# A two-layer hybrid model on one core: where the second batch's projection stands in a list of side work

## Chip, core and metric

The kernel runs on one core of a Trainium2 chip. The metric is device time in microseconds (us); shown are the median, the lowest and the highest of the runs of a kernel. A profiled execution gives the trace: every instruction with its start and duration, the DMAs, and the clock that TensorE was granted. Engines are named as in the profile: PE is TensorE's matmuls, PEld its weight loads, DVE VectorE, ACT ScalarE, POOL GpSimd, SP the queue that issues most DMAs.

## What is computed

The input x is 2 batches of 1024 tokens of width 128, held as 16 tiles of 128 tokens (tiles 0 to 7 are batch 0, 8 to 15 batch 1). Eight blocks are applied one after the other, each as x = x + block(layernorm(x)). The last four matter here; the change lies in the seventh and eighth:

```python
x = x + _L1_attn_a_ref(_layernorm(x, axis=-1), ...)   # linear attention
x = x + _L1_ffn_ref(_layernorm(x, axis=-1), Wg, Wu, Wd)
x = x + _L1_attn_b_ref(_layernorm(x, axis=-1), ...)   # the head softmax
x = x + _L1_ffn_ref(_layernorm(x, axis=-1), Wg, Wu, Wd)
```

The head softmax has 16 heads of 8 dimensions, and its softmax runs over the heads (axis 1), not over the keys:

```python
dp = jnp.einsum('bhqd,bhkd->bhqk', q, k) * SCALE
attn = jax.nn.softmax(dp, axis=1)
w_avg = jnp.einsum('bhqk,bhkd->bhqd', attn, v)
```

The expert block sums, over 8 experts, (silu(x Wg) * (x Wu)) Wd with a middle width of 512. It works token by token, so any group of tokens can be done as soon as their own input is final. The head softmax mixes the tokens of one batch and needs the keys and values of the whole batch.

## The kernel before, in words

`first_layer` does the first five blocks and, beside the end of them, the expert block for tokens of batch 0. `experts_ffn(g, w, [2])` does it for tiles 8 to 11. Then comes `heads_and_experts(g, w, [6, 7], [0, 1, 2, 3, 4, 5])`, and last `experts_ffn(g, w, [3])`, the eighth block for tiles 12 to 15.

**The loop.** `heads_and_experts` walks over 128 blocks: batch b, tile of queries qb, tile of keys kb, the keys innermost (L1120). The order of instructions on every engine is the order of the calls (`manual_schedule`). Work on a block is spread over five iterations of the loop at L1137, which runs i from -1 to 131:

- L1030 (PE): the scores of all 16 heads for block i+1, into h_s.
- L1041 and L1047 (DVE): the largest score over the heads, and the scores less it, into h_e.
- L1050 (ACT): the exponentials in place, in two halves.
- L1056 (DMA from SP) and L1060 (adding DMA from POOL): the upper eight heads are added on the lower eight in flight, giving h_e2. (The page gives both names as h_e.)
- L1065 (PE): the eight sums are added up by matmuls with the identity, into h_pd. L1070 (DVE): the reciprocal.
- L1075 (POOL): h_a = exponentials times reciprocal. L1081 (PE): the weighted values into h_po.

After the eighth key tile of a query tile the result is copied (L1176), projected (L1145) and added to x (L1154), and `finished` goes up by one.

**The expert stream.** In the same iterations runs the expert block on chunks of two tiles (`ExpertStream`). Chunks 6 and 7 (tiles 12 to 15) still belong to the sixth block, and the head softmax of batch 1 needs them; chunks 0 to 5 (tiles 0 to 11) belong to the eighth and need the head softmax of their own tiles. Opening a chunk is five steps: statistics (L62, L63 on DVE), root (L66, ACT), inverse (L69, DVE), application (L73, POOL), and transposes (L863, PE), which put 32 units, one for each expert and quarter of the middle width, into `ex.units`. In each iteration `ex.products()` takes two units and multiplies by Wg and Wu (L879), `ex.gates()` does the silu (L886, ACT), and in the next iterations `ex.multiply()` (L894, DVE), `ex.outputs()` (L905, PE) and `ex.add()` (L914, DVE) finish them. L905, L1145 and L1065 share one bank, h_pd, which has a single buffer.

**The projection.** `preparation(b)` normalizes the eight tiles of batch b and makes its queries, keys and values. Its steps are four of statistics and an inverse (DVE), a root (ACT), four applications (L73, POOL), eight on PE (two each of transposes L986, keys L1001, queries L992, values L1007, each with what follows on ACT or DVE) and two biases (L979, POOL). Batch 0's is done ahead of the loop, beside chunk 6. Batch 1's has to be done by the time block 64 begins: its scores are issued in iteration 63, and `spread(1)` (L1023) at the end of iteration 66 uses its values.

**The list.** `side` is an ordered list of such openings and the projection of batch 1. Each entry has a number that `finished` has to reach. `aside(place)` is called four times in an iteration, with "pe", "act", "dve" and "pool", and does the next step of the current entry if it belongs to that place. When an entry is used up, the next is taken only if `finished` has reached its number and `ex.units` holds no more than 8 units. A step of place "pe" stands in place of `ex.products()`: in such an iteration no units are taken. Nothing in the list overtakes.

After the loop, a `while` loop (L1179) takes what is left, two units in a round, with nothing beside them.

Of the kernel before, what the change touches and what calls it, by code (L numbers as in the profile page):

```python
# [927 lines left out]
def heads_and_experts(g, w, first, second):  # L928
# [4 lines left out]
    with ExitStack() as es:  # L933
# [24 lines left out]
        ex = ExpertStream(g, w, ework, ps_e)  # L958
        qzs, kTs, vs = {}, {}, {}

        def preparation(b):

            xb = g.x[:, b * TPB : (b + 1) * TPB, :]
            ln = StagedNorm(g, xb, TPB, "h")
            u = seq.tile([P, TPB, D], F32, name="h_u", bufs=1)
            uT = seq.tile([P, L], F32, name="h_uT", bufs=1)
            qzs[b] = seq.tile([P, K, L], F32, name="h_qz")
            kTs[b] = seq.tile([P, L], F32, name="h_kT")
            vs[b] = seq.tile([P, TPB, D], F32, name="h_v", bufs=1)
            for t in range(0, TPB, 2):  # L970
                yield "dve", lambda t=t: ln.stats((t, t + 1))
            yield "act", ln.root
            yield "dve", ln.inverse
            for t in range(0, TPB, 2):
                yield "pool", lambda t=t: ln.apply(u, (t, t + 1))


            def bias(t):
                nc.gpsimd.tensor_add(  # L979
                    xb[:, t : t + 4, :], xb[:, t : t + 4, :], w["b_proj2"].unsqueeze(1).to_broadcast([P, 4, D])  # L980
                )

            def transposes(n):
                pt = ps_e.tile([P, 4, P], F32, name="e_pgu")
                for t in range(4):
                    nc.tensor.transpose(pt[:, t, :], u[:, 4 * n + t, :], g.ident)  # L986
                nc.scalar.copy(uT[:, bass.ts(n, 512)], pt.rearrange("p a b -> p (a b)"))

            def query(n):
                cols = bass.ts(n, 512)  # L990
                pm = ps_e.tile([P, 4, P], F32, name="e_pgu").rearrange("p a b -> p (a b)")
                nc.tensor.matmul(pm, w["w_qkv2"][:, 0:P], uT[:, cols], start=True, stop=True)  # L992
                for k in range(K):
                    nc.scalar.activation(  # L994
                        qzs[b][:, k, cols], pm, AF.Identity, bias=keep_b[:, k : k + 1], scale=keep[:, k : k + 1]
                    )

            def key(n):
                cols = bass.ts(n, 512)
                pm = ps_e.tile([P, 4, P], F32, name="e_pgu").rearrange("p a b -> p (a b)")  # L1000
                nc.tensor.matmul(pm, w["w_qkv2"][:, P : 2 * P], uT[:, cols], start=True, stop=True)  # L1001
                nc.scalar.activation(kTs[b][:, cols], pm, AF.Identity, bias=w["b_qk2"][:, 1:2])

            def value(n):
                pv = ps_e.tile([P, 4, P], F32, name="e_pgu")
                for t in range(4):
                    nc.tensor.matmul(  # L1007
                        pv[:, t, :], uT[:, bass.ts(4 * n + t, P)], w["w_qkv2"][:, 2 * P : 3 * P], start=True, stop=True
                    )
                nc.vector.tensor_add(  # L1010
                    vs[b][:, 4 * n : 4 * n + 4, :], pv, w["b_v2"].unsqueeze(1).to_broadcast([P, 4, D])
                )

            for step in (transposes, key, query, value):
                for n in range(2):
                    yield "pe", lambda step=step, n=n: step(n)
            for t in (0, 4):
                yield "pool", lambda t=t: bias(t)
# [69 lines left out]

        side = [(2 * c + 2, ex.opening(c)) for c in second]
        side.insert(2, (0, preparation(1)))
        side = [(0, ex.opening(c)) for c in first[1:]] + side
        finished, current, head = 0, None, None

        def aside(place):

            nonlocal current, head
            while True:
                if head is None:  # L1100
                    if current is None:
                        if not side or side[0][0] > finished or len(ex.units) > 8:
                            return False
                        current = side.pop(0)[1]
                    head = next(current, None)
                    if head is None:
                        current = None
                        continue
                break
            if head[0] != place:  # L1110
                return False
            step, head = head[1], None
            step()
            return True
# [7 lines left out]
        with tc.manual_schedule(engines=ALL):  # L1122
# [14 lines left out]
            for i in range(-1, n + 4):  # L1137
# [9 lines left out]
                if not aside("pe"):  # L1147
                    ex.products()
# [3 lines left out]
                if oT is not None:  # L1152
                    xt = g.x[:, finished, :]
                    nc.vector.tensor_add(xt, xt, pd[:, 2, :])  # L1154
                    finished, oT = finished + 1, None
                aside("act")
                ex.gates()
                if i + 1 < n:
                    e_[i + 1] = exponentials(heads, m)
                    e2_[i + 1] = lower(e_[i + 1])  # L1160
                aside("dve")
                if 0 <= i - 1 < n:
                    d_[i - 1] = denominators(e2_.pop(i - 1))
# [115 lines left out]
def kernel(ctx: ExitStack, tc: tile.TileContext, d: dict, out: bass.AP):  # L1279
# [36 lines left out]
    layer0.close()  # L1316
    experts_ffn(g, w, [2])
    heads_and_experts(g, w, [6, 7], [0, 1, 2, 3, 4, 5])
    experts_ffn(g, w, [3])

# [67 lines left out]
```

## Time and profile before

| what | value |
|---|---|
| median of 3 runs (lowest to highest) | 2319.74 us (2317.05 to 2331.03) |
| profiled execution: its own time | 2328.53 us |
| profiled execution: span of its instructions | 2326.8 us |
| busy in the span: PE, DVE, ACT, POOL | 2015.9, 1629.0, 1183.5, 854.9 us |
| loop of the head softmax: first to last L1041 | 1307.8 to 2190.2 us |
| last expert stage: its first transpose (L96) | 2237.37 us |
| the part from 1308 us on, of the span | 1019 us |

The span is counted from the first instruction to the last; 1.7 us of the execution lie around it. All times of single instructions below are of the profiled execution, in us from the start of its span. The head softmax with its loop and the last expert stage are somewhat under half of the span. A busy PE is not PE at its peak, since the ends of matmuls are modelled, but a gap in it is a gap.

### The profile page before, as it was taken

To read this page: it belongs to the slowest core of one execution; us is meant where nothing else is said; L and a number is where in the kernel's file an instruction comes from. 1 tells how busy PE (TensorE), PEld (TensorE's weight loads), DVE (VectorE), ACT (ScalarE), POOL (GpSimd) and SP (SyncE) were. 2 spreads that over 40 slices of the span, in tenths; PEclk is the share of its full clock that TensorE was granted. 3 is DMA by queue.
4 is the path that set the end of the run, shared out by engine and by line. 5 is a ranking of instruction groups with operands and counts; after the bars stand their busy time and mean duration, and the time that the engine had idled before them with its cause. 6 is when DMAs were issued, how large, how long until landed. Compare 5 with 4: busy or idle time off the path is not lost. (4 is left out here: it accounts for less than half of the span.)

```text
span 2326.8 us, 36810 instructions
## 1 busy us (share of the span) xinstructions
PE 2015.9 (87%) x15152; PEld 1184.5 (51%) x15152; DVE 1629.0 (70%) x1988; ACT 1183.5 (51%) x1486; POOL 854.9 (37%) x460
## 2 busy tenths in 40 slices
PE   7779988887987748789698799999977999999999
PEld 4323344323334313235345577677755777777754
DVE  5851047788974659993423699899978999999732
ACT  1014521353643458764322576777735777777632
POOL 0001100033320000000102277878788787877700
PEclk9789997878998879899799899999989999999999
DMA  3000000076732067640000266566556665665500
GB/s 86 1 1 1 2 1 1 18 190 152 185 93 89 4 159 184 162 106 0 1 1 0 64 153 157 145 152 157 146 150 152 157 155 155 153 162 146 137 5 5
DMA packets 72647, 220.19 MB, mean 95 GB/s; under 512 B 9056, under 2 KB 19744, under 8 KB 72352
## 3 DMA queue, kind: packets, MB, share of 16 engines
q1 hardware_dynamic: 53584, 149.40, 21.5%
q0 software_dynamic: 18432, 67.12, 15.3%
q8 instruction: 119, 1.95, 0.3%
q10 hardware_dynamic: 464, 1.33, 0.3%
q14 instruction: 48, 0.39, 0.1%
HBM read 78.35 MB, written 5.24 MB: 36 GB/s over the span
## 5 line engine op out<-in xcount | busy, mean ns | idle before, releaser
L1075 POOL TENSOR_TENSOR h_a<-h_e,h_r 128x2048 f32<-128x2048 f32 x128 | 581.4, 4542 | 130.4 <-PE h_po L1081 93.9
L1041 DVE TENSOR_REDUCE h_m<-h_s 128x128 f32<-128x2048 f32 x128 | 293.2, 2291 | 73.2 <-PE h_s L1030 73.1
L1065 PE MATMUL h_pd<-h_e,ident 128*128 128x128 f32 x2048 | 267.4, 285 | 43.4 <-DMA h_e<-h_e 29.6
L1050 ACT ACTIVATE h_e<-h_e 128x1024 f32<-128x1024 f32 x256 | 256.5, 1049 | 89.6 <-DVE h_e L1047 71.4
L1047 DVE TENSOR_TENSOR h_e<-h_s,h_m 128x2048 f32<-128x2048 f32 x128 | 292.6, 2286 | 3.4 <-DVE h_m L1041 1.7
L1065 PEld LDWEIGHTS h_pd<-h_e,ident 128*128 128x128 f32 x2048 | 244.6, 196 | 87.3 <-DVE x_res L914 41.5
L304 POOL TENSOR_SCALAR_AFFINE_SELECT a_pT<-a_pT 128x256 f32<-128x256 f32 x128 | 97.2, 775 | 431.4 <-ACT a_pT L301 430.5
L301 ACT ACTIVATE a_pT<-a_st 128x1024 f32<-128x1024 f32 (+1 forms) x192 | 145.1, 808 | 139.1 <-PE a_st L291 137.0
L886 ACT ACT_TABLE_LOAD x105 | 134.7, 1283 | 150.5 <-PE e_pgu L879 150.3
L806 DVE TENSOR_TENSOR e_h<-e_sg,e_pu 128x512 f32<-128x512 f32 x128 | 87.0, 686 | 176.5 <-PE e_pu L802 151.2
L243 DVE TENSOR_REDUCE a_nm<-a_s 128x2 f32<-128x1024 f32 (+7 forms) x144 | 168.4, 1218 | 48.5 <-PE a_s L234 24.2
L804 ACT ACTIVATE e_sg<-e_pg 128x512 f32<-128x512 f32 x128 | 76.0, 596 | 192.5 <-PE e_pg L801 192.3
L825 PE MATMUL e_po<-e_h,Wd 128*128 128x512 f32 x256 | 139.4, 630 | 39.4 <-DVE e_h L806 39.3
L225 PE MATMUL a_s<-a_latT,a_qT 32*128 32x512 f32 (+3 forms) x768 | 128.7, 650 | 49.4 <-DVE a_nm L243 47.6
L905 PEld LDWEIGHTS h_pd<-Wd,e_h 128*128 128x128 f32 x1024 | 125.5, 191 | 90.1 <-DVE e_h L894 76.8
L1030 PE MATMUL h_s<-h_qz,h_kT 32*128 32x512 f32 x1024 | 148.5, 649 | 19.5 <-DVE h_e L1047 13.9
L879 PE MATMUL e_pgu<-e_uT,Wg 128*128 128x256 f32 x512 | 154.1, 383 | 4.0 <-ACT h_qz L994 2.1
L905 PE MATMUL h_pd<-Wd,e_h 128*128 128x128 f32 x1024 | 149.1, 287 | 5.9 <-DVE e_h L894 3.7
L879 PE MATMUL e_pgu<-e_uT,Wu 128*128 128x256 f32 x512 | 152.3, 379 | 0.0
L1060 POOL DMA_DIRECT2D h_e<-h_e x128 | 113.6, 887 | 104.0 <-DVE h_m L1041 48.8
L638 DVE TENSOR_TENSOR_SCAN s_h<-s_a,s_h 128x1024 f32<-128x1024 f32 x64 | 147.4, 2303 | 5.9 <-ACT s_a L606 1.7
L801 PE MATMUL e_pg<-e_uT,Wg 128*128 128x512 f32 x256 | 141.9, 638 | 2.1 <-ACT e_uT L794 2.1
(246 smaller groups left out, 3191.6 us busy)
## 6 DMA issues: line engine op xcount, KB each, us to landing
h_e<-h_e SPq DMA_DIRECT2D x128, 512.0 KB, 4.0
h_e<-h_e POOLq DMA_DIRECT2D x128, 512.0 KB, 4.6
s_a<-s_steps SPq DMA_DIRECT2D x64, 512.0 KB, 4.8
s_h<-s_steps SPq DMA_DIRECT2D x64, 512.0 KB, 6.3
s_steps<-s_delta SPq DMA_DIRECT2D x4, 512.0 KB, 2.6
s_steps<-s_dtx SPq DMA_DIRECT2D x4, 512.0 KB, 3.4
Wg<-in_Wg_dram SPq DMA_DIRECT2D x8, 256.0 KB, 6.0
Wu<-in_Wu_dram SPq DMA_DIRECT2D x8, 256.0 KB, 5.9
```

The costliest lines, as they stand in the source:

```text
L243: nc.vector.tensor_reduce(nm[:, half, i, h : h + together], s[:, :, :n], AX.X, ALU.max, negate=True)
L301: nc.scalar.activation(pT[:, :, off:], s[:, :, off:], AF.Exp)
L638: nc.vector.tensor_tensor_scan(h, a, h, 0.0, ALU.mult, ALU.add)
L801: nc.tensor.matmul(pg, w["Wg"][:, e, f], opened[n], start=True, stop=True)
L879: nc.tensor.matmul(pgu[:, k, :], w[name][:, e, f], uT, start=True, stop=True)
L905: nc.tensor.matmul(po[:, t, :], h[:, bass.ts(t, P)], self.w["Wd"][:, e, fc, :], start=(k == 0), stop=(k == 1))
L1030: nc.tensor.matmul(s[:, j, :].rearrange("p (k q) -> p k q", k=K), kTs[b][quad, bass.ts(kb, P)], qzs[b][quad, :, bass.ts(qb, P)], start=Tru ...
L1041: nc.vector.tensor_reduce(m, heads.rearrange("p h q -> p q h"), AX.X, ALU.max)
L1047: nc.vector.tensor_sub(e, heads, m.unsqueeze(1).to_broadcast([P, H, P]))
L1050: nc.scalar.activation(eh, eh, AF.Exp, scale=scale)
L1065: nc.tensor.matmul(pd, g.ident, e2[:, k, :], start=(k == 0), stop=(k == 7))
L1075: nc.gpsimd.tensor_mul(a, e, r.unsqueeze(1).to_broadcast([P, H, P]))
```

## The change

Each entry of the list gets a second number, the units that may be left over when it is taken (it was 8 for all). The projection of batch 1 moves from behind chunk 1 to behind chunk 0, and its number is 24; all openings keep 8.

```diff
-        side = [(2 * c + 2, ex.opening(c)) for c in second]
-        side.insert(2, (0, preparation(1)))
-        side = [(0, ex.opening(c)) for c in first[1:]] + side
+        side = [(2 * c + 2, 8, ex.opening(c)) for c in second]
+        side.insert(1, (0, 24, preparation(1)))
+        side = [(0, 8, ex.opening(c)) for c in first[1:]] + side
...
-                        if not side or side[0][0] > finished or len(ex.units) > 8:
+                        if not side or side[0][0] > finished or len(ex.units) > side[0][1]:
                             return False
-                        current = side.pop(0)[1]
+                        current = side.pop(0)[2]
```

So the list was: chunk 7, chunk 0 (from 2 finished tiles on), chunk 1 (from 4), projection, chunks 2 to 5 (from 6, 8, 10, 12). It becomes: chunk 7, chunk 0 (from 2), projection with up to 24 units left, chunk 1 (from 4), chunks 2 to 5 as before. The instructions are the same; their places in the loop differ.

## Prediction

> **What bounds the kernel now.** I read the page first. Its chain of waits over the whole span is spread over many stages, so it does not say what a list of side work is worth. The groups then show which engine each part of the head softmax occupies, and from there I went to the stage itself: busy time by stretches, the timeline of single iterations, and the chain in the last 150 us.
>
> Busy time of each engine in stretches (columns: busy us and instruction counts of PE, PEld, DVE, ACT, POOL; granted TensorE clock; DMA share; GB/s):
>
> ```profile
> 1480.00:1660.00 180.00, 176.59 (x1861) 136.18 (x1860) 164.41 (x162) 134.98 (x158) 140.72 (x55) 1.00 0.60 153
> 1709.00:1726.00 17.00, 11.83 (x116) 8.76 (x116) 10.87 (x7) 4.57 (x6) 12.84 (x7) 0.76 0.54 135
> 1726.00:1782.00 56.00, 43.67 (x478) 31.39 (x478) 44.95 (x28) 23.80 (x31) 45.07 (x19) 0.92 0.56 147
> 2224.00:2237.00 13.00, 12.25 (x78) 11.04 (x76) 6.09 (x15) 3.28 (x9) 0.00 (x0) 1.00 0.00 0
> ```
>
> The first line is the loop with expert units in every iteration: PE is busy 98% at full clock. The second and third are where the loop has run out of units and only the projection of the second batch stands beside it: PE falls to 70 and 78%, and the clock to 0.76 and 0.92. The fourth is after the loop: PE alone, no DMA, POOL idle. I call iterations with units loaded and those without light. Iteration i (from -1) is found by its L1041, which works on block i+1; "row i" is the time from its L1041 to the next.
>
> A loaded iteration in the timeline:
>
> ```profile
> 1967.07 1.16 PE L905 MATMUL h_pd<-Wd,e_h 128*128 128x128 f32 x8
> 1968.07 0.60 PE L879 MATMUL e_pgu<-e_uT,Wg 128*128 128x256 f32 x2
> 1969.88 2.05 PE L1065 MATMUL h_pd<-h_e,ident 128*128 128x128 f32 x16
> 1971.86 1.08 PE L1081 MATMUL h_po<-h_a,h_vz 128*32 128x128 f32 x32
> 1972.88 1.14 PE L1030 MATMUL h_s<-h_qz,h_kT 32*128 32x512 f32 x8
> 1973.94 1.16 PE L905 MATMUL h_pd<-Wd,e_h 128*128 128x128 f32 x8
> ```
>
> From L905 to L905 is 6.87 us with no gap: 1.0 outputs, 1.8 units (L879), 2.0 denominators, 1.0 weighing, 1.1 scores. PE sets the loaded row. A light one, with one projection step:
>
> ```profile
> 1740.02 1.13 PE L1001 MATMUL e_pgu<-h_uT,w_qkv 128*128 128x512 f32 x2
> 1742.24 2.02 PE L1065 MATMUL h_pd<-h_e,ident 128*128 128x128 f32 x16 [1.10 <-DMA h_e<-h_e]
> 1744.19 1.08 PE L1081 MATMUL h_po<-h_a,h_vz 128*32 128x128 f32 x32
> 1745.20 1.14 PE L1030 MATMUL h_s<-h_qz,h_kT 32*128 32x512 f32 x8
> ```
>
> Here 6.27 us pass, with PE waiting 1.10 for the sum in flight (h_e by DMA): DVE's 5.5 us of two reductions and a reciprocal, and that DMA, set the light row. So 2.8 us of expert work put into a light row costs only 6.87 - 6.1 to 6.3 = 0.6 to 0.8 us. After the loop the same work is bare; the chain shows one such round, 2.62 us (2226.34 to 2228.96):
>
> ```profile
> 2226.34 0.89 PE h_pd L905 x8
> 2227.23 1.73 PE e_pgu L879 x8
> 2228.96 0.89 PE h_pd L905 x8
> ```
>
> **What the change does, counted.** I ran the list by hand with the rules of the code (two units an iteration, a step of place "pe" in their stead, `finished` one up every eight). Before, chunk 1 is opened at i=35 and fed from i=38, the projection starts at i=50 when 8 units are left, they end at i=54, and i=55 to 69 have none: 15 light iterations. Chunk 2 waits for the projection, and so each chunk after it. Chunk 5 comes to PE at i=117 and 10 of its units are left when the loop ends at i=131. The traces confirm each of these places (L879 stops and starts there). After: chunk 0 is open at i=21, its 24th unit from the end is reached at i=25, and the projection runs i=25 to 41 (statistics 25 to 28, root 29, applications 29 to 32, eight PE steps 33 to 40, biases 40 and 41). Only i=33 to 40 have no new units; the 10 left resume at i=41, chunk 1 opens at i=42 with 6 left, and from there no chunk is late. The last unit goes at i=130. Five loaded iterations more, none of the five bare rounds.
>
> **The moved steps, priced.** No instruction is added or removed, none of the moved steps issues a DMA, and SP's issues keep their order with the blocks; what moves on SP is the write of the first 512 rows, ready some nine rows later, in a loaded row. The second such write, at 2045 in a loaded row of 6.88, cost nothing, so I take nothing (if SP stalled on it, the h_e copies would queue behind it: up to 1 us).
>
> Rows 50 to 71 of before hold projection and refill: 6.99, 7.19, 6.99, 7.07, 6.88, 6.87, 6.88, 10.22, 6.90, 8.26, 6.12, 6.27, 6.73, 8.10, 7.78, 6.10, 6.75, 6.74, 6.40, 6.86, 6.92, 6.36, in all 155.4. The same 22 roles after are rows 25 to 46; each takes the nearest row of before:
> - 25 to 29, statistics (four instructions, 0.9 us of DVE, hidden behind PE but for 0.12) and the root, already in loaded rows before: 6.99, 6.99, 7.19, 6.99, 6.88 = 35.0.
> - 30 to 32, applications on POOL, now beside units. POOL then has 0.88 + 1.6 to 2.0 + 4.52 = 7.0 to 7.4 against 6.87; behind them on POOL stands the next h_a, which PE's L1081 waits for. 6.95, 6.95, 7.0 = 20.9 (7.4 each would add 1.3).
> - 33 and 34, transposes while outputs drain, as rows 55 and 56: 6.9 each.
> - 35, first key step with a finished tile: 6.6 (row 67 has 6.74 with statistics).
> - 36 to 40, as 61 to 65: 6.3, 6.7, 8.1, 7.8, 6.1. The 8.1 and 7.8 stay: L1010 stands before L1041 on DVE and waits for PE.
> - 41 to 46, refill and opening of chunk 1, as rows 1 (5.96, here with a bias of 1.56 on POOL), 3, 36, 37, 38, 39, where a kind has several rows their middle: 6.5, 6.9, 7.2, 7.0, 6.9, 6.2.
> In all 152.0. Elsewhere before has four openings in loaded rows (chunks 1, 3, 4, 5) and after too (2 to 5), and 80 rows of the same kinds: **the loop -3.4**. The bounds are -8 (no stall at all) and +2 (stalls like rows 57 and 59 come back, and POOL's 1.3).
>
> **The end.** Before, the last stage's first transpose L96 starts at 2237.37, after the bare rounds, though its input has been ready since 2223.9. After, nothing is left for PE but one pair of outputs, and L96 follows that normalization: L1154 at 2217.87, statistics, root with its table load, applications from 2220.78. The same opening without cover is in the trace before the third expert stage:
>
> ```profile
> 1153.07 3.12 POOL L73 TENSOR_SCALAR e_u<-x_res,e_mv,e_rs 128x128 f32<-128x128 f32 x4 [2.05 <-DVE ln_st L62]
> 1157.45 2.08 PE L801 MATMUL e_pg<-e_uT,Wg 128*128 128x512 f32 x2 [0.73 <-ACT e_uT L794]
> 1159.31 1.92 PE L802 MATMUL e_pu<-e_uT,Wu 128*128 128x512 f32 x2
> ```
>
> 4.38 us from L73 to L801, so L801 at 2220.78 + 4.38 = 2225.2 in place of 2238.67: -13.5 (five rounds of 2.62 are 13.1). [...] The row: these matmuls took 2.08 and 1.92, those at 2238.67 and after 1.13 and 1.02; the granted clock from 1150 to 1162 was 0.57, and at 2237 to 2242 it is 1.00 because the bare rounds had kept PE busy. By the row, the first three pairs take 4.67 in place of 2.68: 2.0 us. [...] **The end -11.5**; bounds -13.5 (clock stays) and -9.5 (two windows cold).
>
> Sum: -3.4 - 11.5 = -14.9. Against the profiled execution (span 2326.8, its own time 2328.5) that is a span of 2311.9 and a time of 2313.6. That execution lies 8.8 above the median of the runs, so the forecast stands on the median: 2319.7 - 14.9 = **2304.8**.
>
> **Rivals.**
> - The stretch keeps its price (0.20). Rows 57 and 59 were long because the clock fell (6.83 us at half rate from 1711.05 and again from 1724.70) after PE waited 3.35 for a DMA. [...]
> - All clean (0.12): light rows without a stall and no cold start, -8 - 13.5 = -21.5, 2298.2.
> - The last stage does not start sooner (0.08): L96 is held by something else than the rounds, such as the memory of the loop being freed late. Only the loop's part is left, 2316. Against it: its other input is ready at 2223.9.
> - Slower (0.03): the clock stays halved through the eight light rows. Row 57 at half rate took 10.2, against my 55.4 for rows 33 to 40: 81.6, +26, in all +11 and 2331. It decides from five such rows on (5 x 3.3 = 16.5 over 14.9). Against it: of 13 light rows before, two were so, and rows 60 to 64 ran at full clock.
>
> My forecast has 0.57 with its own range 2299 to 2310. A measurement of this kernel can tell about 1% from no change (the three runs span 0.6%). Faster by over 1% means under 2296.5: part of the clean case and of scatter, 0.08. Slower means over 2342.9: 0.03. Within: 0.89. The range takes in the stretch that keeps its price, the last stage not sooner and most of the clean case, widened by the runs' own scatter of some 3 us: 2294 to 2317.
>
> **What would show it.** Right: L879 in every row from 41 to the loop's end; no row above 9 us in 33 to 40; no bare round after the last L1154; L96 some 6 us after it; first L801 near 2 us at a clock near 0.5. Wrong: POOL's h_a late in rows 30 to 33 with PE waiting on it; several half-rate windows between rows 33 and 41; L96 still over 15 us after L1154; loaded rows over 6.87.

## The result, and the profile after

The changed kernel takes 2317.99 us in the median (2308.21 to 2326.60), the kernel before, run beside it, 2323.63 (2314.59 to 2333.81). The ratio is 0.9966, with a 95% interval of 0.9951 to 0.9982: about 8 us faster, between 4 and 11. Forecast were 14.9, a ratio of 0.9936. The sign was right, the size about half, and the time lies 1 us outside the range that was given. (The kernel before took 3.9 us more here, over 22 runs, than in the first three runs, on which the forecast stood.)

The profiled execution has a span of 2319.9, 6.9 less than before. A profile is a single execution: up to the first L1041, in code that the change doesn't touch, the nine profiles (below) without matmuls put ahead of the loop take 1294.9 to 1307.8. So the ratios come from many runs, and the profiles are compared by stretches. Both traces are cut at the same places here; "row" and "loaded" as in the prediction:

| stretch (us) | before | after | difference | forecast |
|---|---|---|---|---|
| start of the span to L1041 of iteration 24 | 1479.1 | 1477.3 | -1.8 | 0 |
| the 22 rows of projection and refill (50 to 71; 25 to 46) | 155.4 | 154.6 | -0.8 | -3.4 |
| the other 80 rows up to 125 | 555.7 | 562.6 | +6.9 | 0 |
| last L1041 to last L1154 | 27.6 | 29.2 | +1.6 | 0 |
| last L1154 to the end of the span | 108.9 | 96.1 | -12.8 | -11.5 |

So the end came nearly as priced, and the loop took some of it back. In the fourth stretch a sum in flight holds L1065 for 2.24 us in after and for 0.51 before. The stretches of after (columns as before: busy us and counts of PE, PEld, DVE, ACT, POOL; clock; DMA share; GB/s):

```profile
1541.00:1597.00 56.00, 43.37 (x499) 30.25 (x500) 45.77 (x30) 24.74 (x31) 45.56 (x19) 0.99 0.62 157
...
1639.00:2195.00 556.00, 537.35 (x5657) 414.34 (x5657) 502.66 (x499) 410.85 (x484) 431.78 (x167) 1.00 0.59 152
...
2229.00:2235.00 6.00, 5.28 (x9) 2.38 (x9) 0.69 (x1) 2.85 (x4) 0.00 (x0) 0.60 0.01 3
```

The first holds the eight light iterations, now at a clock of 0.99 (0.76 and 0.92 before). The second is one unbroken stretch of loaded rows, and its PE is busy 96.6%, not the 98.1% of the stretch shown for before: 3.4% of the time it is not. The third is the start of the last stage, at a clock of 0.60. The end in the timeline of before:

```profile
2217.87 0.28 DVE L1154 TENSOR_TENSOR x_res<-x_res,h_pd 128x128 f32<-128x128 f32 x1
...
2218.80 1.28 ACT L66 ACT_TABLE_LOAD   x1
...
2220.78 3.13 POOL L73 TENSOR_SCALAR e_u<-x_res,e_mv,e_rs 128x128 f32<-128x128 f32 x4 [7.70 <-DVE e_rs L69]
...
2237.37 0.63 PE L96 MATMUL e_pg<-ident,e_u 128*128 128x128 f32 x4 [0.60 <-DVE x_res L914]
```

And in that of after:

```profile
2222.47 1.28 ACT L66 ACT_TABLE_LOAD   x1
...
2223.80 0.28 DVE L1154 TENSOR_TENSOR x_res<-x_res,h_pd 128x128 f32<-128x128 f32 x1
...
2225.36 3.12 POOL L73 TENSOR_SCALAR e_u<-x_res,e_mv,e_rs 128x128 f32<-128x128 f32 x4 [6.34 <-DVE e_rs L69]
...
2226.20 0.33 PE L96 MATMUL e_pg<-ident,e_u 128*128 128x128 f32 x1 [0.84 <-POOL e_u L73]
...
2229.73 2.08 PE L801 MATMUL e_pg<-e_uT,Wg 128*128 128x512 f32 x2 [0.72 <-ACT e_uT L794]
...
2231.59 1.91 PE L802 MATMUL e_pu<-e_uT,Wu 128*128 128x512 f32 x2
```

No bare round is left. From L73 to L801 are 4.37 us (4.38 were taken from the earlier stage), and L801 and L802 take 2.08 and 1.91, as the cold opening there did. The end gained 1.3 us more than forecast because L73 now follows L1154 after 1.56 us (2.91 before). With its last silu at 2221.15, ACT loads the root's table ahead of L1154 (2222.47) and not behind it (2218.80 before).

Some loaded rows wait, row 97 for one:

```profile
1986.65 0.87 POOL L1060 DMA_DIRECT2D h_e<-h_e  x1 [0.36 <-issue]
...
1989.01 2.29 DVE L1041 TENSOR_REDUCE h_m<-h_s 128x128 f32<-128x2048 f32 x1
...
1993.16 2.02 PE L1065 MATMUL h_pd<-h_e,ident 128*128 128x128 f32 x16 [1.40 <-DMA h_e<-h_e]
...
1994.83 0.88 POOL L1060 DMA_DIRECT2D h_e<-h_e  x1 [1.85 <-DMA h_e<-h_e]
...
1997.34 2.29 DVE L1041 TENSOR_REDUCE h_m<-h_s 128x128 f32<-128x2048 f32 x1 [0.55 <-PE h_s L1030]
```

The adding DMA issued at 1986.65 came late, L1065 waited 1.40 for it, and the row (L1041 to L1041) took 8.33 in place of 6.87. The DMA queues in that stretch, 1987 to 1993 (packets, MB, share; then issue and us to landing):

```profile
q0 software_dynamic: 144, 0.52, 46.9%
...
q8 instruction: 1, 0.02, 1.0%
...
h_e<-h_e POOLq DMA_DIRECT2D x1, 512.0 KB, 6.4
```

The adding DMA took 6.4 us (4.6 in the median of the page), and one packet of the instruction queue fell into its flight. Among the rows that wait are 80, 81, 95, 97, 111 and 114 in after, and 93, 109, 114, 115 and 125 before. In the plain loaded rows between 24 and 125 (no other step in them), what goes beyond 6.87, or 7.09 where a tile is finished, sums to 4.3 us before (60 rows) and 9.8 after (60 rows).

### The profile page after: what moved, and what is told of

It reads as the page before. It is cut to its first block, busy times and chain, and to the rows that moved or that the text cites. A ratio compares the mean times of both kernels' runs of the same rounds, so it can differ in the third digit from the quotient of the medians.

```text
span 2319.9 us, 36808 instructions
## 1 busy us (share of the span) xinstructions
PE 2009.7 (87%) x15152; PEld 1178.6 (51%) x15152; DVE 1626.4 (70%) x1988; ACT 1197.2 (52%) x1497; POOL 855.5 (37%) x460
## 3 DMA queue, kind: packets, MB, share of 16 engines
q8 instruction: 119, 1.95, 0.4%
## 5 line engine op out<-in xcount | busy, mean ns | idle before, releaser
L1041 DVE TENSOR_REDUCE h_m<-h_s 128x128 f32<-128x2048 f32 x128 | 293.2, 2291 | 71.9 <-PE h_s L1030 71.8
L1065 PE MATMUL h_pd<-h_e,ident 128*128 128x128 f32 x2048 | 262.7, 282 | 43.3 <-DMA h_e<-h_e 30.0
L1065 PEld LDWEIGHTS h_pd<-h_e,ident 128*128 128x128 f32 x2048 | 240.7, 193 | 85.7 <-DVE x_res L914 45.6
L225 PE MATMUL a_s<-a_latT,a_qT 32*128 32x512 f32 (+3 forms) x768 | 122.4, 615 | 51.5 <-DVE a_nm L243 49.9
```

The lines of the kernel that those rows point to most:

```text
L1041: nc.vector.tensor_reduce(m, heads.rearrange("p h q -> p q h"), AX.X, ALU.max)
L1065: nc.tensor.matmul(pd, g.ident, e2[:, k, :], start=(k == 0), stop=(k == 7))
```

## The experiments

Two theories stood after the first pair. **A**, later sharpened to **C**: which loaded rows wait is decided by something other than the list, first thought to be scatter between executions, then where in PE's program the packets of the instruction queue q8 come (one to 254.7 of PE's records over the span of before; taken for loads of its code, last section). **B**: the new list itself makes loaded rows wait. All kernels, by their profile and their ratio to the kernel before (in us; "excess" is the sum over plain rows just described):

| run | list | matmuls put ahead | rows 24 to 125 | excess, plain rows | last L1154 to end | ratio (95%) |
|---|---|---|---|---|---|---|
| first profile | before | 0 | 711.1 | 4.3 | 108.9 | 1 |
| first profile | after | 0 | 717.2 | 9.8 | 96.1 | 0.9966 (0.9951 to 0.9982) |
| e1_before_again | before | 0 | 716.3 | 7.3 | 109.0 | 1.0007 (0.9990 to 1.0024) |
| e2_after_again | after | 0 | 717.2 | 12.4 | 95.4 | 0.9974 (0.9960 to 0.9989) |
| e3_sooner_only | sooner, 8 left | 0 | 708.9 | 3.2 | 109.0 | 0.9999 (0.9981 to 1.0016) |
| e4_left_only | old place, 24 left | 0 | 718.7 | 11.1 | 96.3 | 0.9972 (0.9957 to 0.9987) |
| f6_before_shift8 | before | 8 | 716.8 | 10.6 | 109.0 | 1.0022 (1.0010 to 1.0034) |
| f1_after_shift8 | after | 8 | 728.1 | 10.9 | 96.7 | 0.9999 (0.9986 to 1.0013) |
| g3_before_shift12 | before | 12 | 714.3 | 8.1 | 109.0 | 1.0029 (1.0018 to 1.0041) |
| g2_after_shift12 | after | 12 | 722.2 | 11.7 | 96.3 | 0.9998 (0.9982 to 1.0015) |
| f8_before_shift16 | before | 16 | 721.1 | 13.4 | 109.0 | 1.0073 (1.0046 to 1.0100) |
| f7_after_shift16 | after | 16 | 716.8 | 8.4 | 95.6 | 0.9982 (0.9968 to 0.9996) |
| f3_before_shift24 | before | 24 | 720.3 | 7.9 | 108.9 | 1.0081 (1.0049 to 1.0114) |
| f2_after_shift24 | after | 24 | 715.9 | 12.4 | 95.3 | 0.9987 (0.9974 to 1.0000) |
| f4_after_warm | after | filler at the end | 715.2 | 9.3 | 98.5 | 0.9972 (0.9958 to 0.9986) |
| f5_after_warm2 | after | filler at the end | 716.7 | 10.9 | 94.2 | 0.9961 (0.9948 to 0.9973) |
| g1_left14 | sooner, 14 left | 0 | 719.0 | 5.9 | 101.1 | 1.0001 (0.9979 to 1.0023) |

**Second profiles of both kernels.** e1:

> The kernel before, unchanged, for a second profile. In the first pair of profiles the end (from the last L1154) fell by 12.8 us as priced, but the loop (first to last L1041) grew by 7.3, nearly all of it in loaded rows that waited for a late adding DMA (L1060, landing over 5.4 us after its issue). Theory A (lottery): which loaded rows wait is scatter between executions; this loop will lie anywhere in 881 to 891 us. Theory B (systematic): loaded rows of the list of before wait less; the loop comes back at 880 to 884. Ratio 1.000 by both.

e2:

> The changed kernel, unchanged, for a second profile. Theory A: loop anywhere in 880 to 891 us, from the last L1154 to the end 96 us again (108.9 before); with a loop near 882 the span would be some 12 us under that of before. Theory B: loop again 888 to 892, with 17 or more adding DMAs over 5.4 us (12 before).

The loop of e1 took 891.2 and that of e2 888.9. The first is against B and at A's upper end; the second fits B. But B had also asked for 17 or more adding DMAs over 5.4 us in e2: there are 11 (16 in e1; 12 and 19 in the first pair). The end is the same to 0.7 us in every profile of a list. But A as first put, pure scatter, fell too: rows 80, 81, 95, 97, 111 and 114 waited again in e2, and 84, 93, 114, 115 and 125 again in e1 (84 with 7.12 and 7.40). Not every row came again (72 of after and 109 of before did not), but most belong to the program.

**The two halves of the change.**

```diff
-        side.insert(1, (0, 24, preparation(1)))
+        side.insert(1, (0, 8, preparation(1)))     # e3_sooner_only
+        side.insert(2, (0, 24, preparation(1)))    # e4_left_only
```

> One half of the change alone: the projection one chunk sooner, but with the old limit of 8 units. By the rules of the list 15 iterations have no new units (38 to 52) and 10 units are left after the loop, as before. If the end is what counts (A and B): from the last L1154 to the end 108 to 110 us, ratio 0.999 to 1.001. If standing sooner is worth something by itself: ratio 0.997 or less with the rounds after the loop still there. Under B its loop is that of before, 880 to 884.

> The other half alone: the projection in its old place behind chunk 1, with up to 24 units left over. Eight iterations without new units (50 to 57), no unit left after the loop. If the end is what counts: from the last L1154 to the end 96 us, ratio 0.995 to 0.9975, the same as the whole change. Under B the loop is 887 to 892, under A anywhere in 880 to 891.

The end in the timeline of e3:

```profile
2213.13 0.28 DVE L1154 TENSOR_TENSOR x_res<-x_res,h_pd 128x128 f32<-128x128 f32 x1
...
2232.64 0.63 PE L96 MATMUL e_pg<-ident,e_u 128*128 128x128 f32 x4 [0.60 <-DVE x_res L914]
```

And in that of e4:

```profile
2222.05 0.28 DVE L1154 TENSOR_TENSOR x_res<-x_res,h_pd 128x128 f32<-128x128 f32 x1
...
2224.44 0.33 PE L96 MATMUL e_pg<-ident,e_u 128*128 128x128 f32 x1 [0.84 <-POOL e_u L73]
```

L96 stands 19.5 us after L1154 in e3, as before, and 2.4 in e4, as after. Standing sooner alone is worth nothing (0.9999); letting units be left over alone is worth the whole change (0.9972 beside 0.9974 for e2). So the gain goes with the emptied end and not with standing sooner. For the loop B had asked for 880 to 884 in e3 and 887 to 892 in e4: they took 887.4, a miss, and 891.7. With e4, three profiles of lists with nothing left show 717 to 719 for rows 24 to 125, and three of lists with ten left 709 to 716: that looked like B, and the next runs were made to tell.

**Moving PE's code against the rows.** In both kernels n small matmuls are issued ahead of the loop, in a bank that is free there; nothing reads them:

```diff
+            spare = ps_d.tile([P, 4, D], F32, name="h_pd")
+            for _ in range(8):
+                nc.tensor.matmul(spare[:, 0, :], g.ident[0:32, :], g.ident[0:32, :], start=True, stop=True)
             spread(0)
```

> The changed kernel with 8 small matmuls (32x128 by 32x128) put on PE just ahead of the loop, so that PE's instructions, and with them the places where the queue of instructions (q8) loads the next piece of PE's code, shift by 32 against the rows; the list is untouched. So far the loaded rows that wait are the same in every profile of one list (80, 81, 95, 97, 106, 111, 114 after; 84, 93, 114, 115, 125 before), and in most of them such a load falls into the flight of the adding DMA. Theory C (place of the code loads): the waiting rows move, and the excess of the loaded rows over 6.87 (10 to 12 us in the lists with no unit left, 3 to 7 in those of before) changes by 2 us or more. Theory B (the list itself makes these rows wait, whatever the code's place): the same rows 80, 81, 95, 97, 111 wait, rows 24 to 125 take 717 to 719 us again.

> The same with 24 such matmuls, a shift of 96 instructions. Theory C: other rows wait than in the changed kernel and than with 8; rows 24 to 125 anywhere in 708 to 720 us. Theory B: rows 80, 81, 95, 97, 111 wait, 717 to 719 us.

> The kernel before with the same 24 matmuls ahead of the loop. Theory C: rows 84, 93, 125 no longer wait and others do; the excess of its loaded rows leaves 3 to 7 us, perhaps up to the 10 to 12 of the changed kernel, and then the difference between the two lists in the loop is gone. Theory B: 3 to 7 us again, rows 24 to 125 at 709 to 716 us.

With 24, rows 80, 81, 95 and 111 of the changed kernel no longer wait, 97 still does, and 82, 84, 91, 98 and 107 are new. In the kernel before, 84, 93 and 125 no longer wait, and 83, 94, 101 and 104 do. With 8, rows 77 and 78 are new, but 95, 97 and 111 wait again and the excess stays at 10.9, so that run by itself is a miss for C. It is one for B too: 728.1 for rows 24 to 125, where B had asked for 717 to 719. Row 97 again, with 16 put ahead (f7, below), where the DMA of 1991.53 took 4.5 us:

```profile
1991.53 0.86 POOL L1060 DMA_DIRECT2D h_e<-h_e  x1
...
1994.06 2.28 DVE L1041 TENSOR_REDUCE h_m<-h_s 128x128 f32<-128x2048 f32 x1
...
1996.73 2.05 PE L1065 MATMUL h_pd<-h_e,ident 128*128 128x128 f32 x16
...
2000.93 2.29 DVE L1041 TENSOR_REDUCE h_m<-h_s 128x128 f32<-128x2048 f32 x1 [0.55 <-PE h_s L1030]
```

No wait stands at L1065, and the row takes 6.87. Same list, same iteration, another place in PE's code.

The partners, and two more shifts:

> The kernel before with 8 small matmuls ahead of the loop, the partner of the changed kernel with 8 (ratio 0.9999). Theory C: the difference of the two lists depends on the place of the code loads, -7 us without a shift, -22 us at 24; here anywhere from -4 to -24, so this kernel has a ratio of 1.001 to 1.010; waiting rows again differ from those of the other shifts. Theory B: the lists differ by 6 to 8 us as without a shift, ratio 1.0025 to 1.0035.

> The changed kernel with 16 small matmuls ahead of the loop (some 4 us of PE by themselves, as 24 took 6.2). Theory C: waiting rows differ again; from the last L1154 to the end 95 to 97 us as always with this list. Ratio 0.996 to 1.001.

> The kernel before with 16, the partner of the one above. Theory C: the mean of the four pairs (0, 8, 16, 24) lies at -10 to -17 us, near the end's -12.5 and the stretch's -1 to -2, and the pair without a shift is only one draw of it. Theory B: this pair too at -6 to -8 us.

> The changed kernel with 12 small matmuls ahead of the loop. Theory C: other rows wait; ratio 0.996 to 1.001. From the last L1154 to the end 95 to 97 us.

> The kernel before with 12, its partner. Theory C: the pair's ratio is anywhere from 0.990 to 0.998 and the mean of the five pairs is 0.993 to 0.9955 (-10 to -16 us). If the pair without a shift is typical and 16 and 24 are special: 0.997.

The added matmuls cost a few us by themselves (24 of them 6.2 us of PE), the same for both partners, so each pair is read by the quotient of its two ratios. They are 0.9974 (0), 0.9977 (8), 0.9969 (12), 0.9910 (16) and 0.9907 (24): -6, -5, -7, -21 and -22 us for one and the same edit of the list. Their mean is 0.9947, -12 us. C's expectation for the mean (-10 to -17) held; B's (each pair at -6 to -8) fell at 16 and 24. What I can't settle is whether -12 is the typical worth. Three of the five lie near -6, and the pair at 12 came out where it was expected "if the pair without a shift is typical and 16 and 24 are special" (0.997). The two partners on which -21 and -22 rest have few runs (7 and 5), though their intervals lie clear of the others. And before's list at 16 and 24 takes 0.7 to 0.8% longer than without a shift, more than its added matmuls and the longer rows of its profiles come to.

Over all 14 profiles of these lists (without fillers and without g1), 1792 adding DMAs: 415 had a packet of q8 start within 4.5 us of their issue. These took 5.38 us in the mean, and 49% took over 5.4; the other 1377 took 4.67, and 1.5% took over 5.4. With the packet 1.5 to 4 us after the issue, the mean is 6.1, and all 80 such DMAs took over 5.4. Of the rows 67 to 125, 36% of those whose DMA met such a packet took over 7.3 us, and 6% of the others. Row 114 is an exception: it takes 7.9 us or more in 13 of the 14 profiles, wherever the code stands, and in several of them no packet of q8 meets its DMA. What holds it is open; it costs much the same in the first pair (8.40 and 8.39).

**The cold clock at the end.**

```diff
+            spare = ps_s.tile([P, J, 512], F32, name="h_s")
+            for _ in range(7):
+                nc.tensor.matmul(spare[:, 0, 0:256], g.ident, kTs[1][:, 0:256], start=True, stop=True)
```

> The changed kernel with 7 matmuls (128x128 by 128x256, 3.0 us at full clock, written to the scores' bank and read by nobody) after the last outputs, so that PE does not stand still while the last normalization runs. If the cold clock at the last stage's start is worth the 2.0 us of the forecast: granted clock 1.00 over the first expert products (0.5 now), the first two L801 in 1.0 to 1.1 us (2.08 now), from the last L1154 to the end 94 us (96.1 now). If the filler delays the transposes instead: L96 later and the end at 96 us or more.

That try told nothing of the clock, since in its timeline POOL waited for the filler's reads:

```profile
2222.43 3.13 POOL L73 TENSOR_SCALAR e_u<-x_res,e_mv,e_rs 128x128 f32<-128x128 f32 x4 [9.48 <-PE h_s L1190]
```

The second reads `w["w_qkv2"][:, 0:256]` in place of `kTs[1][:, 0:256]`:

> The filler again (7 matmuls after the last outputs, 3.0 us), now reading a weight that stays in memory to the end. In the first try it read the keys of batch 1, whose memory the last stage's normalized input takes over, so that the applications L73 waited for the filler (2222.43 in place of about 2219.3) and the question stayed open. If a cold clock costs 2.0 us at the last stage: L73 about 1.6 us after the last L1154, clock 1.00 over the first expert products, from the last L1154 to the end 94 us (96.1 without filler). If transposes with 0.45 us gaps let the clock fall all the same: first L801 2.1 us again and 96 us.

Its end in the timeline:

```profile
2214.60 0.28 DVE L1154 TENSOR_TENSOR x_res<-x_res,h_pd 128x128 f32<-128x128 f32 x1
...
2215.99 3.19 PE L1190 MATMUL h_s<-w_qkv,ident 128*128 128x256 f32 x14
...
2219.28 0.63 PE L96 MATMUL e_pg<-ident,e_u 128*128 128x128 f32 x4
...
2220.63 1.12 PE L801 MATMUL e_pg<-e_uT,Wg 128*128 128x512 f32 x2 [0.72 <-ACT e_uT L794]
```

And the stretch of its first expert products:

```profile
2220.00:2226.00 6.00, 5.37 (x13) 2.50 (x14) 1.38 (x2) 3.65 (x5) 0.00 (x0) 1.00 0.01 3
```

The clock is 1.00, L801 takes 1.12, and from L1154 to the end are 94.2 us, against 95.3 to 96.7 in seven profiles with nothing left and no filler (mean 95.9): 1.7 us for a filler that nobody reads. L801 starts no sooner (6.03 us after L1154, 5.93 in after), so the gain lies in the faster products. Its ratio, 0.9961, is the best of all; against the changed kernel the intervals overlap, so that it beats it is shown for the end and not for the whole.

**Leaving some rounds for the shade of the normalization.**

```diff
-        side.insert(1, (0, 24, preparation(1)))
+        side.insert(1, (0, 14, preparation(1)))
```

> The projection behind chunk 0 with up to 14 units left over in place of 24. By the rules of the list it runs from i=30, twelve iterations without new units, and 4 units are left after the loop, two rounds of 2.6 us. They should lie beside the last normalization (5.9 us from L1154 to L801 in the changed kernel) and keep the clock at 1.00. If so: from the last L1154 to the end 94 to 96 us although two rounds stand there; if rounds after the loop always count: 96 + 5 = 101 us. The light rows more save about 4 x 0.7 us in the loop. Ratio 0.994 to 0.998, the place of the code loads being a draw of +-5 us.

The end in its timeline:

```profile
2218.32 0.28 DVE L1154 TENSOR_TENSOR x_res<-x_res,h_pd 128x128 f32<-128x128 f32 x1
...
2221.24 3.14 POOL L73 TENSOR_SCALAR e_u<-x_res,e_mv,e_rs 128x128 f32<-128x128 f32 x4 [7.71 <-DVE e_rs L69]
...
2228.21 1.16 PE L905 MATMUL h_pd<-Wd,e_h 128*128 128x128 f32 x8 [0.51 <-DVE x_res L914]
...
2229.97 0.63 PE L96 MATMUL e_pg<-ident,e_u 128*128 128x128 f32 x4 [0.60 <-DVE x_res L914]
```

It fell: 101.1 us, as if the rounds counted in full. The input was ready at 2224.4, but the last rounds' way from units over silu and product to outputs and their sum ended at 2229.8. A round takes 2.6 us of PE, and the last one needs two more steps to drain. Its light stretch was long too (159.5, with five half-rate windows between 1591 and 1667), and the ratio is 1.0001.

## Why the prediction was right and where it failed

**The end** (-11.5, bounds -13.5 to -9.5) was right: -12.3 to -13.6 in seven profiles of lists with nothing left. Both terms held: 4.37 us from L73 to L801, and cold products at 2.08 and 1.91. The cold start, 2.0 by the row, measured 1.7 in f5. The second cold window of the bound at -9.5 is shown by no run: the seven ends stand at -12.3 or beyond, and in after the last stage starts in one stretch at half rate, 6.83 us from 2226.98. What was not priced is that L73 follows L1154 1.35 us sooner. (Of the signs, "L96 some 6 us after it" was off: L96 stands 2.4 us after L1154, L801 5.9.)

**The moved steps.** The count was right to the iteration: eight light ones at 33 to 40, the last units at 130. The prices of single rows mostly held: 33 to 40 took 55.7 against 55.4. Missed were rows 29 and 30 (7.25 and 7.60 against 6.88 and 6.95) and the refill (41 to 46: 42.2 against 40.7). Over all profiles without g1 and the fillers the 22 rows take 153.3 to 157.4 with ten units left and 152.5 to 159.4 with none. So the -3.4 is not there beyond scatter: the means are 155.2 and 155.1, which in the number is the rival in which the stretch keeps its price. What that rival and the upper edge of 2310 stood for, 4.7 us of stalls as in rows 57 and 59 (10.22 and 8.26 against 6.9 each), is not shown by the profile of after: the clock was 0.99 over the light rows and none took over 9 us.

**The step that failed** is "Elsewhere before has four openings in loaded rows ... and after too ..., and 80 rows of the same kinds: the loop -3.4". The rows are of the same kinds, and yet the same kind did not cost the same: those 80 took +6.9 us in the first pair and +3.5 in the second (561.2 in e1, 564.7 in e2). The profile had the reason in it. I put 6.87 on a loaded row from one without a wait, and let the longer ones (93, 109, 125) stand as equal on both sides without asking what they wait for. They wait for an adding DMA, and such a DMA lands later when a packet of q8 starts in its flight (5.38 us against 4.67 in the mean), and where those packets fall against the rows moves with the list: row 97 holds one after (1989.01 to 1997.34) and none before (1987.83 to 1994.71). A term of zero there should have been a term of plus or minus some 6 us: over the places tried, rows 24 to 125 take 708.9 to 721.1 with ten units left and 715.2 to 728.1 with none. One kernel in one place moves too (711.1 and 716.3 in the two profiles of before), so not all of that width is the place. With it the range would have held the time. The warning stood in the prediction's own list ("loaded rows over 6.87"), without a price.

That it is the place more than the list is best seen in rows 72 to 125, which are loaded rows with three openings in either list. In the two pairs with nothing put ahead the changed list takes 7.0 and 7.1 us more there; it takes 2.9 more with 8, 0.4 with 12 and 0.9 with 24, and 7.7 less with 16. Each is one profile or two; the mean over the five places is 0.7: as a mean the term of zero was not far off, and what it lacked was its width.

The baseline added to the miss. Of the 13.2 us between 2304.8 and 2317.99, 3.9 are the kernel before, whose median of three runs was low; that part is scatter. The rest is the change, worth 8 (5.6 by the two medians) in place of 14.9.

Whether the fuller list also waits more in itself is open. The mean excess of plain rows is 8.2 us over six places with ten left and 10.9 over six with none; 2.7 us in a spread of some 4.

## What to carry to other kernels

Work that is left over after a loop is worth what it takes there bare, less what it costs in rows that have room, and the worth of the emptied end was forecast here from rows of the trace to 1.3 us. Before a difference of a few tenths of a per cent in a long unrolled loop is put down to the edit, shift the code by a few harmless instructions in both kernels and measure again; here the ratio of one edit came out between 0.991 and 0.998 that way. And when a round is left to lie in the shade of something, count its whole way to the last write, not its time on the busiest engine.

## What the runs showed of the hardware that was not expected

An adding DMA lands later when a packet of q8, a queue that the page calls instruction, starts in its flight. In the loop of before q8 moves a packet about every 12.3 us (nine intervals between 1837.0 and 1947.3), and the 119 of its span have 1.95 MB, 16.4 KB each. They keep step with PE's records: a loaded row has 36 matmul calls, 144 records of loads and matmuls, and the sixteen rows of before from 1842.87 to 1953.11 hold 2287 records and nine packets, one to 254.1. Over its whole span there are 30304 records of PE and PEld, one packet to 254.7. And the rows that wait are others when PE's instructions are moved, so I take the packets for loads of PE's code; no view names the engine that they serve. No wait of PE is put down to such a packet itself (rows 76, 78 and 80 of before hold one each and take 6.87 or 6.88). But a 512 KB adding DMA in whose flight one starts lands 0.7 us later in the mean (5.38 against 4.67) and 1.4 later in the worst phase (6.1), and where PE has less slack than that it stands still (1.40 us in row 97 above). Waiting rows recur at a distance of sixteen: 93, 109, 125 before; 81, 97, 113 and 95, 111 after.
